# A state-space layer's schedule: one ScalarE table for exp and ln, decays made ahead of Silu, step products and key work at other places

## The chip, the cores and the metric

The kernel runs on one core of a Trainium2 chip. The metric is device time in microseconds (us) from launch to end, the median of three runs. TensorE is PE in the profile (its weight loads PEld), VectorE is DVE, ScalarE is ACT, GpSimd is POOL; SyncE (SP) issues most of the DMAs.

## The reference, cut to what matters

Four layers, each added to `x` (4 x 512 x 512): a selective state-space layer (SSM), a mixture of experts, a cross attention, and a ternary feed-forward. The change is in the first. For each batch `b` of four, with `ctx` (4 x 512 x 256):

```
xs    = in_proj_w @ ctx[b].T                        # 512 channels x 512 steps
u     = silu(causal_conv4(xs, conv_w) + conv_b)
dt_lo, Bm, Cm = split(x_proj_w @ u)                 # 16 rows each
delta = softplus(dt_proj_w @ dt_lo + dt_proj_b)
A     = -exp(A_log)                                 # 512 channels x 16 states
state[e, n] = state[e, n] * exp(delta[e, t] * A[e, n]) + delta[e, t] * u[e, t] * Bm[n, t]
y[e, t]     = sum_n state[e, n] * Cm[n, t] + D[e] * u[e, t]
x[b] += (y * silu(layernorm(x[b]))).T
```

The cross attention also takes `ctx`: its keys (`ctx @ Wk`, 16 heads of 128, RMS normalised) and values (`ctx @ Wv`). Much of these is computed during the SSM, where the kernel has room.

## The kernel before, in words

`ssm_phase` works with channels on the partitions: four chunks of 128 channels (`c`) per batch, 512 time steps along the row. The 16 states of a chunk are done in pairs (`i`, 0 to 7), so a batch is 32 *slots* (`s = c * 8 + i`), and the loop `for q, (b, c, i) in enumerate(seq)` goes through 128 slots, `q` in all. One slot is:

- `inputs` on POOL: `dBu = bb * du`, for two slots ahead (L488; three buffers);
- `decays` on ACT: `dA = exp(delta * A)`, two instructions, one slot ahead (L497; two PSUM buffers, each free when the slot that used it is done on DVE);
- `scan` on DVE: one recurrence over both states (L511), then the product with `cb`, on DVE or, for i = 0, 2 and 4, on POOL (L512; `hc`, three buffers, free when PE has summed them);
- `sums` on PE for the slot before: `hc` is transposed and summed into `yT` (L517). At the second pair of the next chunk or so, `result` multiplies by the gate `gzT` (L551, DVE) and adds to `x_all` (L553, POOL).

Beside it, `ahead(b + 1, s)` prepares the next batch: in slots 0 to 15 the convolution on PE (L304, filters `wcvc` loaded by `load_wcv`, two buffers) and its eviction as `u` (L309); in slot 17 Silu of the four `u` (L376) and layer-norm statistics (`stats`, L380; `norm` on POOL); in 18 and 19 the projection `pd` (L404) and its eviction `xd`; in 20 to 28 four times the *steps*, one for each chunk: product `pdt` (L424) on PE, Abs, Exp and 1+ on ACT (`steps_a`, L428 to L430), Ln (`steps_ln`, L437), and the sum to `delta` on DVE with `du` on POOL (`steps_b`, L443 to L448). softplus(v) is max(v, 0) + ln(1 + exp(-|v|)), with a correction for rounding. In slot 28 Silu of the layer-normed `x` gives the gates `gz` (L397); in 26 to 31 `rows` loads the broadcast `bb` and `cb`. Batch 0 does its own first step ahead of the loop and the other three in slots 2 to 13.

The same slots carry the attention's values (a product `pv` in every odd slot, L470, evicted as `v` in the next even one, L476) and keys: `task` is the product `pk` (L1094), `evict` takes it twice (square into tile `e`, scaled into tile `wt`; L1103, L1104), `squares` sums the squares into `kpss` (L1114), `take` evicts that (L1126) and stores it.

All this is under a manual schedule: every engine runs its instructions in the order in which the program writes them, and waits for those of other engines. A table load on ACT (ACT_TABLE_LOAD) is put in by the compiler wherever a function is not in the loaded set; Exp and Ln are each loaded from a set of their own. PSUM banks are shared by tags: `pa` by `pd`, `pdt`, the gate's transposes `pgz` and key tiles; `pin` by the convolution, key products, and `ln` from batch 1 on (for batch 0 `ln` is in SBUF). After the SSM comes `route`, whose first statistics (L158) reuse the SSM's memory.

Of the kernel before, what the change touches and what calls it, by code (L numbers as in the profile page):

```python
# [17 lines left out]
F32 = mybir.dt.float32  # L18
# [5 lines left out]
AF = mybir.ActivationFunctionType  # L24
# [199 lines left out]


@with_exitstack
def ssm_phase(ctx, cm, x_all, w, kv, dr):
# [11 lines left out]
    KC = CTX // P  # L239
    NP = DS // 2  # L240
    R = 64

# [37 lines left out]
    nc.scalar.dma_start(dtT[0:DR, :], w["dt_proj_wT"])  # L280
    nc.scalar.dma_start(dtT[DR:, :], w["dt_proj_b"])
    nc.scalar.activation(negA, negA, AF.Exp)

# [54 lines left out]
    def silu_0(c):  # L338
        nc.scalar.activation(st[0]["u"][c], st[0]["u"][c], AF.Silu)


# [32 lines left out]
    def silu_u(b):  # L374
        for u in st[b]["u"]:
            nc.scalar.activation(u, u, AF.Silu)  # L376

    def stats(b, c):
# [14 lines left out]
    def silu_gz(b):  # L393
        s = st[b]
        for c in range(NC):
            gz = pool[5].tile([P, S], F32, name="gz")
            nc.scalar.activation(gz, x_all[:, b * NC + c, :], AF.Silu, bias=s["nmr"][:, c:c + 1],  # L397
                                 scale=s["rstd"][:, c:c + 1])
            s["gz"].append(gz)

    def project(b):
# [17 lines left out]

    def steps_a(b, c):  # L420

        s = st[b]
        pdt = s["pdt"] = ps.tile([P, S], F32, name="pdt", tag="pa")
        nc.tensor.matmul(pdt, dtT[:, c * P:(c + 1) * P], s["xd"][0:DR + 1, :], start=True,  # L424
                         stop=True)
        e, wt = (pool[1].tile([P, S], F32, name=n) for n in ("e", "wt"))
        s["e"], s["wt"] = e, wt
        nc.scalar.activation(e, pdt, AF.Abs)  # L428
        nc.scalar.activation(e, e, AF.Exp, scale=-1.0)
        nc.scalar.activation(wt, e, AF.Identity, bias=cm.ones[:, 0:1])  # L430

    def steps_ln(b):

        s = st[b]
        s["ln"] = (pool[5].tile([P, S], F32, name="ln", tag="gz") if b == 0 else
                   ps.tile([P, S], F32, name="ln", tag="pin"))
        nc.scalar.activation(s["ln"], s["wt"], AF.Ln)  # L437

    def steps_b(b, c):

        s = st[b]
        e, wt, ln = s["e"], s["wt"], s["ln"]
        nc.vector.scalar_tensor_tensor(e, wt, 1.0, e, ALU.subtract, ALU.subtract)  # L443
        nc.vector.tensor_tensor(e, ln, e, ALU.subtract)
        delta = pool[5].tile([P, S], F32, name="delta")
        nc.vector.scalar_tensor_tensor(delta, s["pdt"], 0.0, e, ALU.max, ALU.add)
        du = pool[5].tile([P, S], F32, name="du")
        nc.gpsimd.tensor_tensor(du, delta, s["u"][c], ALU.mult)  # L448


        nc.gpsimd.memset(delta[:, 0:1], RESET)
        s["delta"].append(delta)
        s["du"].append(du)
# [36 lines left out]

    def decays(q):
        if q < len(seq):
            b, c, i = seq[q]
            dAs[q] = pda.tile([P, 2, S], F32, name="dA")
            for j in range(2):
                n = 2 * i + j
                nc.scalar.activation(dAs[q][:, j, :], st[b]["delta"][c], AF.Exp,  # L497
                                     scale=negA[:, c, n:n + 1])
# [56 lines left out]
    def ahead(b, s):  # L555

        if s % 4 == 0 and 4 <= s <= 16:
            take_conv(b, s // 4 - 1)
        if s < 16:
            conv(b, s // 4, (s % 4 * 2, s % 4 * 2 + 1))  # L560
        if s in (4, 8):
            load_wcv(b, s // 4 + 1)
        if s == 17:
            silu_u(b)
            for c in range(NC):
                stats(b, c)
            norm(b)
        if s == 18:
            project(b)
        if s == 19:  # L570
            take_project(b)
        if s in (22, 24, 26, 28):
            steps_b(b, (s - 22) // 2)
        if s in (20, 22, 24, 26):
            steps_a(b, (s - 20) // 2)
        if s in (21, 23, 25, 27):
            steps_ln(b)
        if s == 28:
            silu_gz(b)
        if s == 20 and b + 1 < B:  # L580
            start(b + 1)
        if s == 20 and b + 1 == B:
            load_ctx(0, again=True)
        if s in (26, 28, 30, 31):
            rows(b, (26, 28, 30, 31).index(s))

    def key_bank(shape, name):
        return ps.tile(shape, F32, name=name, tag="pin" if name == "pk" and keys.wide else "pa")  # L590

# [4 lines left out]
    def key_steps(b, s, ends):  # L596

        if b > 0 and not ends and s == 0:
            keys.take()
        if b < B - 1:  # L600
            for j, at in enumerate((14, 17, 29) if b == 0 else (3, 6, 11, 14, 17, 29)):
                if not ends and s == at - 3:
                    keys.load(j, j + 1, pool[2], "k_w")
                if not ends and s == at + 3:
                    keys.take()
                if ends and s == at:
                    keys.wide = at > 16
                    keys.task(b + 1, j)
                if ends and s == at + 1:
                    keys.evict()  # L610
                if ends and s == at + 2:
                    keys.squares()
        if b == B - 2 and ends and s in (18, 22):
            h = s - 18
            keys.load(h, h + HG, pool[2], "wcvc")
        if b == B - 1:
            h = s // 2
            if not ends and s % 2:
                keys.take()

            if ends and s == 31:
                keys.squares()
            if ends and s % 2:
                keys.evict()
            if ends and s % 2 == 0:
                if s < 30:
                    keys.squares()
                keys.wide = True
                keys.task(0, h)
                if h in (HG, 2 * HG):  # L630
                    keys.load(h + HG, h + 2 * HG, pool[2], "wcvc")

    def start(b):
        load_ctx(b)
        load_wcv(b, 0)
        load_wcv(b, 1)

# [29 lines left out]
    norm(0)  # L667
    steps_a(0, 0)
    steps_ln(0)
    steps_b(0, 0)  # L670
    decays(0)
    inputs(0)
    inputs(1)
# [3 lines left out]
    for g in range(1, DS // NG):  # L677
        rows(0, g)
    SL = NC * NP
    for q, (b, c, i) in enumerate(seq):  # L680
# [10 lines left out]
        if q % SL == 8 and b + 1 < B:  # L691
            load_x(b + 1)
        if q in (4, 6, 13):
            steps_b(0, len(st[0]["du"]))
        if q in (2, 4, 11):
            steps_a(0, len(st[0]["du"]))
        if q in (3, 5, 12):
# [14 lines left out]
        last = (b + 1) % B, q % SL // 2  # L712
        sums(q - 1)
        key_steps(b, q % SL, True)
    sums(len(seq) - 1)
    take_values(*last)
    keys.take()
    keys.squares()
    keys.take()
# [1563 lines left out]
```

## Time and profile before

Three runs: 2748.58, 2750.00 and 2751.31 us. The profiled execution took 2754.55 us, and its span from first to last instruction is 2752.8.

| stretch of the profiled execution | us |
|---|---|
| before the first scan | 40.2 |
| slots 0 to 15 / 16 to 31 of batch 0 (preparing batch 1) | 74.3 / 78.4 |
| slots 0 to 15 / 16 to 31 of batch 1 | 62.6 / 78.4 |
| slots 0 to 15 / 16 to 31 of batch 2 | 62.3 / 80.0 |
| batch 3, to route's first statistics | 113.4 |
| experts, attention, feed-forward | 2163.2 |

A row of the profile's groups names the line, engine, operation and tiles (out<-in), then shapes and count, busy us and mean ns of one, and the engine's idle time ahead of them with what ended it. A row of waits names who waited for whom, us in total, times, and the longest. A row of the timeline has start, duration, engine and line. Times in the text without another word are us on the profile's own clock.

### The profile page before, as it was taken

What the parts mean: (1) busy time and instruction counts of PE and PEld (TensorE: products, weight loads), DVE (VectorE), ACT (ScalarE), POOL (GpSimd) and SP (SyncE); (2) the same over time, 40 slices, a digit from 0 to 9 for tenths busy, and PEclk for the clock granted to TensorE, in tenths of its full rate; (3) what the DMA queues carried; (4) which work ended last, traced back from release to release, by engine and by line L of the source; (5) the groups of instructions that cost most, each with busy time, mean ns of one, the idle gap of its engine ahead of it and who ended that gap; (6) DMA issues with size and microseconds to landing.
All of it is one profiled execution on the core that took longest, in us unless ns stands there. A gap on an engine that the chain in (4) does not pass through costs nothing. (4 is left out here: it accounts for less than half of the span.)

```text
span 2752.8 us, 30001 instructions
## 1 busy us (share of the span) xinstructions
PE 2545.1 (92%) x10158; PEld 1441.3 (52%) x10158; DVE 1486.0 (54%) x2570; ACT 1275.9 (46%) x2371; POOL 1170.6 (43%) x1121
## 2 busy tenths in 40 slices
PE   5989897976799999999998799999999999999997
PEld 2545454643456666666674455445555554555543
DVE  5887877966432234334423555545665666544445
ACT  6676757743323222222322344445555555555543
POOL 4888887952333244444433423223431443111212
PEclk8979797986899999999999899999999999999999
DMA  6253535322556566879976344324322443221200
GB/s 244 82 201 102 196 103 181 128 78 80 190 187 199 162 216 222 267 264 339 311 235 204 116 134 135 96 88 126 119 92 81 126 126 103 78 81 53 63 31 20
DMA packets 198543, 403.11 MB, mean 146 GB/s; under 512 B 30563, under 2 KB 72099, under 8 KB 194288
## 3 DMA queue, kind: packets, MB, share of 16 engines
q1 hardware_dynamic: 155758, 247.76, 26.9%
q0 software_dynamic: 40576, 153.19, 17.5%
q8 instruction: 83, 1.36, 0.2%
q14 instruction: 76, 0.62, 0.1%
q10 hardware_dynamic: 2050, 0.18, 0.1%
HBM read 319.13 MB, written 81.92 MB: 146 GB/s over the span
## 5 line engine op out<-in xcount | busy, mean ns | idle before, releaser
L1848 DVE TENSOR_REDUCE mx<-psc 128x1 f32<-128x512 f32 x256 | 176.7, 690 | 458.1 <-PE psc L1845 454.8
L1194 PE MATMUL pg<-xT,wg 128*128 128x284 f32 (+12 forms) x1536 | 403.1, 407 | 1.7 <-ACT xT L1181 1.1
L1194 PEld LDWEIGHTS pg<-xT,wg 128*128 128x128 f32 x1536 | 284.5, 195 | 82.7 <-issue 32.0
L1851 ACT ACTIVATE e<-psc,mx 128x512 f32<-128x512 f32 x256 | 176.0, 687 | 313.5 <-DVE mx L1848 313.2
L488 POOL TENSOR_TENSOR dBu<-bb,du 128x1024 f32<-128x1024 f32 x128 | 299.5, 2360 | 26.5 <-DVE dA L511 19.8
L1845 PE MATMUL psc<-kT,qT 128*128 128x512 f32 x512 | 267.0, 603 | 1.0 <-ACT qT L1839 1.0
L1135 POOL DMA_INDIRECT xg<-xn_dram,tok x168 | 172.2, 1025 | 221.6 <-PE pt L1178 179.2
L1872 PE MATMUL po<-eT,v 128*128 128x512 f32 x512 | 233.2, 598 | 9.4 <-ACT eT L1866 9.4
L1811 PE MATMUL pq<-Wq,xnT 128*128 128x512 f32 x512 | 233.3, 599 | 0.7 <-issue 0.7
L1881 PE MATMUL px<-Wo,oT 128*128 128x512 f32 x512 | 231.9, 596 | 0.0
L511 DVE TENSOR_TENSOR_SCAN dA<-dA,dBu 128x1024 f32<-128x1024 f32 x80 | 183.1, 2289 | 56.8 <-ACT dA L497 46.3
L1865 PEld LDWEIGHTS pet<-ident,e 128*128 128x128 f32 x1024 | 127.8, 142 | 146.2 <-issue 120.1
L1822 POOL TENSOR_SCALAR qms<-qms 128x4 f32<-128x4 f32 x64 | 25.0, 391 | 411.5 <-DVE qms L1820 410.7
L497 ACT ACTIVATE dA<-delta,negA 128x512 f32<-128x512 f32 x256 | 176.5, 692 | 18.1 <-DVE hc L512 12.0
L470 PE MATMUL pv<-Wv,ctxb 128*128 128x512 f32 x256 | 148.0, 708 | 28.6 <-ACT v L476 28.6
L517 PEld LDWEIGHTS yT<-ident,hc 128*128 128x128 f32 x1024 | 130.0, 153 | 83.0 <-issue 57.8
L1239 DVE COPY yo<-po 128x512 f32<-128x512 f32 x68 | 47.0, 691 | 231.9 <-PE po L1228 231.8
L1872 PEld LDWEIGHTS po<-eT,v 128*128 128x128 f32 x512 | 96.8, 191 | 136.7 <-issue 116.6
L1865 PE MATMUL pet<-ident,e 128*128 128x128 f32 x1024 | 155.3, 275 | 7.2 <-DVE e L1857 7.2
L1735 POOL DMA_INDIRECT yg<-y_dram,pos x124 | 124.1, 1001 | 87.3 <-issue 63.1
L517 PE MATMUL yT<-ident,hc 128*128 128x128 f32 x1024 | 145.2, 292 | 11.1 <-POOL hc L512 6.4
L1135 POOL DMA_INDIRECT wd<-down,widx x64 | 63.1, 986 | 216.1 <-PE po L1228 182.2
(354 smaller groups left out, 4489.0 us busy)
## 6 DMA issues: line engine op xcount, KB each, us to landing
y_dram<-yo SPq DMA_DIRECT2D x110, 256.0 KB
bb<-bc_dram SPq DMA_DIRECT2D x16, 1024.0 KB
cb<-bc_dram SPq DMA_DIRECT2D x16, 1024.0 KB
v_dram<-v SPq DMA_DIRECT2D x64, 256.0 KB
k_dram<-k_kT SPq DMA_DIRECT2D x64, 256.0 KB
Wq<-Wq SPq DMA_DIRECT2D x16, 1024.0 KB
kT<-k_dram SPq DMA_DIRECT2D x64, 256.0 KB
rk<-r_dram SPq DMA_DIRECT2D x64, 256.0 KB
```

The costliest lines, as they stand in the source:

```text
L488: nc.gpsimd.tensor_tensor(dBus[q], st[b]["bb"][i // 2][:, j:j + 2, :], st[b]["du"][c].unsqueeze(1).to_broadcast([P, 2, S]), ALU.mult)
L497: nc.scalar.activation(dAs[q][:, j, :], st[b]["delta"][c], AF.Exp, scale=negA[:, c, n:n + 1])
L511: nc.vector.tensor_tensor_scan(*flat, 0.0, ALU.mult, ALU.add)
L517: nc.tensor.matmul(yT[:, lc, :], t[:, lc * P:(lc + 1) * P], cm.ident, is_transpose=True, start=first and lc == 0, stop=last, skip_group_ch ...
L1135: nc.gpsimd.indirect_dma_start(out=t[0:n, :], out_offset=None, in_=table, in_offset=bass.IndirectOffsetOnAxis(ap=index, axis=0))
L1194: nc.tensor.matmul(pg[:, 0:n], s["wg"][:, c, m * P:(m + 1) * P], s["xT"][:, c, 0:n], start=c == 0, stop=c == NC - 1)
L1811: nc.tensor.matmul(pq.rearrange("p h d -> p (h d)"), xnTs[b * NC + i][:, c, :], s["Wq"][:, c, :], start=c == 0, stop=c == NC - 1)
L1845: nc.tensor.matmul(pscore, st[b, g]["qT"][:, h, i * P:(i + 1) * P], ks[n], start=True, stop=True)
L1848: nc.vector.tensor_reduce(mx, pscore, AX.X, ALU.max, negate=True)
L1865: nc.tensor.transpose(pt[:, kc, :], e[:, kc * P:(kc + 1) * P], cm.ident)
L1872: nc.tensor.matmul(po, v[:, kc, :], eT[:, kc, :], start=kc == 0, stop=kc == KB - 1)
L1881: nc.tensor.matmul(px, oTs[j * HG + h][:, i * P:(i + 1) * P], st[b, g]["Wo"][:, h, :], start=h == 0, stop=h == HG - 1)
```

## The change

- `tables` loads the set `natural_log_exp_and_others`, which has both Exp and Ln, at the start and after each group of Silu; the compiler then puts in no load between Exp and Ln.
- `steps_a` loses its product, which moves to `dt`, issued a slot earlier: for the first chunk at the end of slot 19, ahead of the key's squares, for the others in slots 21, 23 and 25 ahead of `values` and `sums`. Relu of `pdt` joins Abs on ACT, so that `pdt` is free after these two; `delta` is then relu + e, on DVE, and no longer max(pdt, 0) + e. 1+ moves from `steps_a` to `steps_ln`.
- `steps_b` moves ahead by a slot, to the end of 21, 23, 25 and 27; `du` stays where it was (`step_du`).
- `decays` of slots 18 and 30 are made at the end of 16 and 28, into SBUF buffers of the filters (tag `wcvc`). `load_wcv` for the next batch moves from slot 20 to the ends of 29 and 31.
- `stats` move from slot 17 to 12 to 15, `norm` to 16, Silu of `gz` from 28 to 29.
- Keys: the tasks of slots 3, 6, 11 and 14 move to 2, 5, 10 and 13; each eviction comes a slot later, at its slot's start, and `take` goes to its slot's end. Banks are chosen by task. In batch 3 evictions move from the end of odd slots to the start of even ones, and the weights of heads 4 to 7 are loaded in slot 6 of batch 3 and not in slot 22 of batch 2.

In experts, attention and feed-forward nothing changes. The core of the diff (beside it: calls of `tables(nc)` after the other Silu groups, the same moves for batch 0 ahead of and in its loop, and the last key's eviction after the loop):

```diff
+def tables(nc):
+    nc.scalar.preload_act_table_set("natural_log_exp_and_others")
...
     def silu_u(b):
         for u in st[b]["u"]:
             nc.scalar.activation(u, u, AF.Silu)
+        tables(nc)
...
-    def steps_a(b, c):
+    def dt(b, c):
+        pdt = st[b]["pdt"] = ps.tile([P, S], F32, name="pdt", tag="pa")
+        nc.tensor.matmul(pdt, dtT[:, c * P:(c + 1) * P], st[b]["xd"][0:DR + 1, :], start=True,
+                         stop=True)
+
+    def steps_a(b):
         s = st[b]
-        pdt = s["pdt"] = ps.tile([P, S], F32, name="pdt", tag="pa")
-        nc.tensor.matmul(pdt, dtT[:, c * P:(c + 1) * P], s["xd"][0:DR + 1, :], start=True,
-                         stop=True)
-        e, wt = (pool[1].tile([P, S], F32, name=n) for n in ("e", "wt"))
-        s["e"], s["wt"] = e, wt
-        nc.scalar.activation(e, pdt, AF.Abs)
-        nc.scalar.activation(e, e, AF.Exp, scale=-1.0)
-        nc.scalar.activation(wt, e, AF.Identity, bias=cm.ones[:, 0:1])
+        pdt = s.pop("pdt")
+        s["e"], s["wt"] = (pool[1].tile([P, S], F32, name=n) for n in ("e", "wt"))
+        s["relu"] = pool[5].tile([P, S], F32, name="delta")
+        nc.scalar.activation(s["e"], pdt, AF.Abs)
+        nc.scalar.activation(s["relu"], pdt, AF.Relu)
+        nc.scalar.activation(s["e"], s["e"], AF.Exp, scale=-1.0)

     def steps_ln(b):
         s = st[b]
+        nc.scalar.activation(s["wt"], s["e"], AF.Identity, bias=cm.ones[:, 0:1])
...
-    def steps_b(b, c):
+    def steps_b(b):
...
-        delta = pool[5].tile([P, S], F32, name="delta")
-        nc.vector.scalar_tensor_tensor(delta, s["pdt"], 0.0, e, ALU.max, ALU.add)
+        delta = s.pop("relu")
+        nc.vector.tensor_tensor(delta, delta, e, ALU.add)
+        s["delta"].append(delta)
+
+    def step_du(b):
+        s = st[b]
+        c = len(s["du"])
+        delta = s["delta"][c]
         du = pool[5].tile([P, S], F32, name="du")
         nc.gpsimd.tensor_tensor(du, delta, s["u"][c], ALU.mult)
...
-    def decays(q):
-        if q < len(seq):
+    def decays(q, early=False):
+        if q < len(seq) and q not in dAs:
             b, c, i = seq[q]
-            dAs[q] = pda.tile([P, 2, S], F32, name="dA")
+            dAs[q] = (pool[2].tile([P, 2, S], F32, name="dA", tag="wcvc") if early else
+                      pda.tile([P, 2, S], F32, name="dA"))
...
     def ahead(b, s):
...
+        if 12 <= s < 16:
+            stats(b, s - 12)
+        if s == 16:
+            norm(b)
         if s == 17:
             silu_u(b)
-            for c in range(NC):
-                stats(b, c)
-            norm(b)
...
-        if s in (22, 24, 26, 28):
-            steps_b(b, (s - 22) // 2)
-        if s in (20, 22, 24, 26):
-            steps_a(b, (s - 20) // 2)
+        if s in (20, 22, 24, 26):
+            steps_a(b)
+        if s in (21, 23, 25):
+            dt(b, (s - 19) // 2)
+        if s in (22, 24, 26, 28):
+            step_du(b)
         if s in (21, 23, 25, 27):
             steps_ln(b)
-        if s == 28:
+        if s == 29:
             silu_gz(b)
...
+    def ahead_ends(b, s):
+        if s in (16, 28):
+            decays((b - 1) * SL + s + 2, early=True)
+        if s in (29, 31) and b + 1 < B:
+            load_wcv(b + 1, (s - 29) // 2)
+        if s == 19:
+            dt(b, 0)
+        if s in (21, 23, 25, 27):
+            steps_b(b)
...
     def key_steps(b, s, ends):
...
-            for j, at in enumerate((14, 17, 29) if b == 0 else (3, 6, 11, 14, 17, 29)):
+            for j, at in enumerate((13, 17, 29) if b == 0 else (2, 5, 10, 13, 17, 29)):
-                if not ends and s == at - 3:
+                if not ends and s == max(at - 3, 0):
                     keys.load(j, j + 1, pool[2], "k_w")
-                if not ends and s == at + 3:
+                if not ends and s == at + 2:
+                    keys.evict()
+                if ends and s == at + 3:
                     keys.take()
                 if ends and s == at:
-                    keys.wide = at > 16
+                    keys.banks = {17: ("pin", "pin"), 29: ("pin", "pa")}.get(at, ("pa", "pa"))
                     keys.task(b + 1, j)
-                if ends and s == at + 1:
-                    keys.evict()
                 if ends and s == at + 2:
                     keys.squares()
```

In the loop `ahead_ends(b + 1, s)` follows `sums(q - 1)` and comes ahead of `key_steps(b, s, True)`.

## The prediction, made before the changed kernel ran

> **What bounds the kernel now.** I first read the busy time by stretch, cut where the SSM's slots show it: the scans number the slots, 32 to a batch; the rows are the two halves of batch 0, of batch 1 and of batch 2, and then batch 3 with its tail. Columns: stretch, its length, busy us of PE, weight loads, DVE, ACT, POOL (with counts), granted clock, DMA share, GB/s.
>
> ```profile
> 40.20:114.50 74.30, 63.22 (x223) 34.09 (x224) 57.00 (x37) 49.26 (x69) 60.31 (x31) 0.88 0.48 179
> 114.50:192.90 78.40, 63.15 (x228) 35.99 (x227) 61.00 (x50) 62.91 (x90) 61.89 (x37) 0.78 0.45 154
> 192.90:255.50 62.60, 62.60 (x278) 37.63 (x277) 49.45 (x29) 33.93 (x58) 54.90 (x25) 1.00 0.43 140
> 255.50:333.90 78.40, 63.45 (x231) 35.55 (x230) 61.02 (x49) 63.16 (x90) 60.53 (x36) 0.78 0.44 156
> 333.90:396.20 62.30, 62.30 (x277) 37.39 (x275) 49.35 (x29) 33.79 (x57) 54.88 (x25) 1.00 0.42 139
> 396.20:476.20 80.00, 64.14 (x228) 35.87 (x227) 61.06 (x50) 62.75 (x90) 60.54 (x36) 0.79 0.43 150
> 476.20:589.60 113.40, 105.59 (x569) 70.99 (x567) 98.40 (x59) 75.57 (x137) 102.38 (x47) 0.99 0.36 121
> ```
>
> A first half (slots 0 to 15, with the next batch's convolution) is PE's: 62.6 of 62.6 at full clock, and its products aren't touched. A second half (16 to 31) belongs to nobody: four engines are each some 61 of 78.4 busy, so about 17 us go in waits. Batch 3 has POOL at 102 of 113, and its slots 112 to 119 take 26.7 us with POOL busy throughout. So the change can win in the three second halves, in batch 0's first half (it holds three of batch 0's own steps) and at the tail.
>
> Then the groups of the SSM's stretch, and the waits of batch 1:
>
> ```profile
> L497 ACT ACT_TABLE_LOAD x23 | 29.5, 1283 | 1.9 <-DVE delta L446 1.5
> L437 ACT ACT_TABLE_LOAD x16 | 20.5, 1283 | 0.2
> L428 ACT ACTIVATE e<-pdt 128x512 f32<-128x512 f32 x16 | 9.6, 598 | 33.1 <-PE pdt L424 33.1
> L488 POOL TENSOR_TENSOR dBu<-bb,du 128x1024 f32<-128x1024 f32 x123 | 287.8, 2361 | 26.5 <-DVE dA L511 19.8 <-DMA bb<-bc_dram 5.5 <-DMA v_dram<-v 1.2
> ```
>
> ```profile
> DVE dA L511 <- ACT dA L497: 16.2, 9, 3.8
> ACT k_sq L1103 <- PE pk L1094: 11.2, 5, 2.5
> ACT e L428 <- PE pdt L424: 6.5, 4, 2.7
> PE pv L470 <- ACT v L476: 8.7, 5, 5.3
> ```
>
> The scans wait for decays (L497); ACT is late with them because it loads tables, and because it stands at the head of its queue for pdt and pk, which PE gives late, itself waiting for ACT's v.
>
> **The table loads.** The program orders have 49 table loads in the SSM before and 17 after: 32 x 1.283 = 41.1 us off ACT. The Trainium skill (ScalarE: Activation LUTs, "What ACT_TABLE_LOAD costs") adds a drain of 1.38 to every load, 2.66 in all, which would make it 85. This trace doesn't show that: at 294.54 a load starts 0.02 after a decay's end, and Ln starts 0.01 after the load. I take 1.3. Added: 16 Relu at some 0.60 (as Abs, L428), 9.6 us.
>
> **The port, which speaks against the change.** The skill (SBUF: State Buffer, "Who interferes with whom") says that a DVE instruction with two SBUF inputs and a GpSimd one that reads SBUF exclude each other for a whole instruction. The timeline of DVE shows it:
>
> ```profile
> 62.48 2.65 DVE L444 TENSOR_TENSOR e<-ln,e 128x512 f32<-128x512 f32 x1
> ...
> 297.59 0.69 DVE L444 TENSOR_TENSOR e<-ln,e 128x512 f32<-128x512 f32 x1
> ```
>
> and so does POOL's:
>
> ```profile
> 64.54 2.79 POOL L512 TENSOR_TENSOR hc<-hc,cb 128x1024 f32<-128x1024 f32 x1
> ...
> 296.98 2.72 POOL L512 TENSOR_TENSOR hc<-hc,cb 128x1024 f32<-128x1024 f32 x1 [1.56 <-DVE hc L511]
> ```
>
> With ln in SBUF (batch 0) L444 stands until POOL's instruction ends at 64.5, 2.65 in place of 0.69; with ln in PSUM (297.59) POOL may run beside it. POOL's hc, 2.35 alone, takes 2.7 to 2.8 where it meets L443 (wt and e, both SBUF). The change makes more of that kind: the delta sum now adds relu and e, both SBUF (L446 read pdt from PSUM, 0.69), and the early decays lie in SBUF, so scans 18 and 30 and the product after scan 30 have two SBUF inputs. Without the rule a delta sum costs 0.7; with it, 0.7 to 3.1. I take the rule, since these rows show it, and place each collision below. Behind a blocked DVE instruction stands the next scan; behind a blocked POOL one, dBu and hc.
>
> **A second half, walked on batch 1's clock.** The durations are those of its timeline: scan 2.25, product L512 1.15, dBu 2.33, hc 2.35, two decays 1.42, Silu of u 2.19, v 0.5, a 512-wide PE product 0.86, sums of a slot 0.87.
>
> Slots 16 to 19. The last convolution ends at 258.7 in both. ACT: u, v at 261.1 (after its product), early decays for 18 to 262.5, load, Silu to 266.1, load, decays 19 to 268.8: scan 19 starts there, before at 269.63. The early decays let scan 18 go ahead, but the next scan meets the same Silu. The four stats (3.4 us of DVE, at 263 to 266.5) move to slots 12 to 15, where PE sets the pace: nothing there, and here they lay beside Silu. Scan 18 is blocked by dBu until 265.9; decays 19 hide it.
>
> Slots 19 to 22. pd shares its bank with the gate's, taken by ACT at 269.3 behind decays 19: pd to 272.7, two sums and values to 276.2, pdt to 277.1 (now in front of kpss), kpss to 277.9. Abs writes tile e, which kpss reads, so it starts at 278.0: before 279.57. So this step gains 1.5, not the slot that it moves. Abs, Relu, Exp, v, key's take, decays 22, Identity, Ln: 283.3. L443 starts at 282.75, meets dBu until 283.5; the sum meets the next dBu from 284.95 to 286.5; delta at 287.2. Scan 22 now stands behind delta, where before it stood ahead. Scan 23: 290.8, before 289.1; with no collision 288.4.
>
> Slots 23 to 31. DVE work: 9 scans, 6 products, three steps (2.1 each), one yg: 34.1 us; before these took 44.8, 9.0 of the rest being the waits for decays. After, decays are in time everywhere: Abs, Relu, Exp, v, Identity, Ln and four decays are 6.5 us of ACT in two slots, against 7.8 to 8.9 of DVE work, and Silu of gz (5.4 with its loads, slot 29) hides behind scans 29 and 30, whose decays are made. Collisions: L443 1.15, 0.3, 0.8; delta sums 0, 1.55, 1.6 (the first finds POOL waiting for scan 24); scan 30 0.3, its product 2.4 (dBu goes between); some 0.5 of waiting for dBu: 8.6. Scan 32: 290.8 + 34.1 + 8.6 = 333.5, before 333.9. With no collisions, 288.4 + 34.1 + 1.4 for POOL = 323.9.
>
> PE, however, starts the next first half earlier. Before, values of slot 29 stood 5.33 for v behind gz's Silu, and a backlog put the first convolution product at 335.33. After, v is taken ahead of Silu, and the last sums, released by product 30 (330.1), and kpss put it at 332.0. As PE sets the first half, that is the gain: **3.3** (9 without collisions).
>
> **Elsewhere.** Batch 0's first half: three steps with six loads. u of slot 4, which the next convolution waits for, comes at 66.5 in place of 69.66 (-3.2), and slot 12's wait of 1.42 falls to some 0.6: **4.0**. The loads off the first step (2.6) are worth nothing: dBu of slot 2 starts at 47.93 after bb's landing. Batch 2's second half: batch 3 has no convolution, so the scans count, **0.4**. Batch 3: POOL's. Keys move within PE's slack (6.2 of 6.6 us in two slots); weights of heads 4 to 7, asked for in slot 6 and wanted in slot 8, may cost 0 to 1; 0 taken. Tail: route's first stats wait for the last k_ms to land (589.63); v now goes ahead of the last key's two evictions: **0.9**.
>
> DMAs moved: the filters of the next batch leave slot 20 for 29 and 31 on SP. The first stands behind one pair of bb and cb (2 MB, 5.1 us at the 407 GB/s of 306 to 311), landing 9 us ahead of its use; the second behind cb of slot 31, landing 9 us ahead. Key weights a slot earlier: some 5 us ahead. 0 taken; if that cover goes, PE waits up to 5 a batch.
>
> **Sum.** 4.0 + 3.3 + 3.3 + 0.4 + 0.9 = 11.9. The profiled execution took 2754.55 (span 2752.8, 1.75 around it): 2742.6. The median of the runs is 4.55 below it: **2738**.
>
> **The rivals.**
> - *Collisions fall in POOL's gaps.* For: one of my four sums does. Against: POOL is 61 of 78 busy in a longer half. 4.0 + 9 + 9 + 10 + 0.9 = 33: 2717.
> - *The gain is given back:* a convolution filter or key weights land late, or cold PE (0.5 in half of each second half) eats the 3.3. 2750.
> - *Slower: the port.* A half holds 11 DVE instructions of two SBUF inputs. If they wait 1.7 us each, nearer a whole POOL instruction (2.36), that is 18.7 for the 10.4 that the walk pays: 8.3 more in each of three halves, 25 less 12, so 13 above the median: 2763. It decides from some 14.4 us per half on (4 more, three times). For: POOL nearly always has one queued. Against: delta sums just behind a scan's product often find POOL waiting for that scan.
> - *The change doesn't do what it says:* excluded for loads, since the program has 17.
>
> **How the numbers follow.** First case 0.50 (2728 to 2748), big gain 0.25, given back 0.11, slower 0.14. A measurement here can tell about 0.2%, 5.5 us. Of the first case 0.05 lies within it: faster 0.70, same 0.16, slower 0.14. Range: down to a part of the big gain, 2711, up to the slower one's edge, 2757.
>
> **What would show it.** 17 table loads, no wait for pdt over 1 us; first halves at 62 to 63 us; second halves at 74 to 76 before PE's restart; delta sums with means of 1.5 or more in three of four; scans 30 and 18 longer than 2.3. A mean of 0.7 for the sums would be the big gain; POOL over 65 in a half, the slower case; waits of L304 for wcvc, the third.

## The result, and the profile after

The changed kernel takes 2739.8 us (median of 11 runs, 2733.1 to 2745.75); the kernel before, on the same chip, 2751.3 (11 runs). The ratio is 0.9956, with a 95% interval of 0.9943 to 0.9969: faster by 0.44%, 11.5 us. The profiled execution took 2741.18 us, with a span of 2738.4, against 2754.55 and 2752.8.

The busy time by stretch, cut at the same scans as before: the two halves of batches 0, 1 and 2, then batch 3 with its tail. Columns: stretch, its length, busy us (and counts) of PE, weight loads, DVE, ACT, POOL, then granted clock, DMA share, GB/s.

```profile
39.40:117.20 77.80, 67.10 (x245) 35.91 (x245) 64.55 (x44) 43.98 (x69) 61.54 (x31) 0.91 0.50 186
117.20:191.00 73.80, 55.34 (x220) 32.14 (x218) 65.88 (x43) 52.19 (x83) 64.23 (x36) 0.84 0.46 157
191.00:254.20 63.20, 63.20 (x272) 37.31 (x273) 52.15 (x37) 36.48 (x61) 57.03 (x26) 1.00 0.43 147
254.20:328.50 74.30, 57.64 (x240) 34.38 (x239) 65.11 (x42) 51.57 (x82) 64.34 (x35) 0.86 0.45 160
328.50:391.10 62.60, 62.60 (x267) 36.66 (x267) 52.13 (x37) 36.59 (x61) 56.98 (x26) 1.00 0.43 144
391.10:465.10 74.00, 59.39 (x239) 35.25 (x238) 65.17 (x41) 51.57 (x82) 64.04 (x35) 0.82 0.48 161
465.10:578.50 113.40, 104.30 (x555) 69.46 (x554) 98.38 (x59) 74.03 (x136) 104.54 (x48) 1.00 0.38 119
```

The second halves went from 78.4, 78.4 and 80.0 to 73.8, 74.3 and 74.0. ACT lost about 11 us of work in each, as it should with the loads gone. But DVE gained 4 to 5 us of busy time in each, and POOL 2 to 4: DVE is now busy for 65 of 74. And batch 0's first half became 3.5 longer.

The groups of the SSM's stretch (engine, operation, count, busy us, mean ns, then the engine's idle time ahead of it and what ended it):

```profile
L228 ACT ACT_TABLE_LOAD x9 | 11.5, 1283 | 5.6 <-DMA v_conv_b<-conv_b 5.5
L443 ACT ACTIVATE e<-pdt 128x512 f32<-128x512 f32 x16 | 9.6, 597 | 44.9 <-DVE delta L462 22.2 <-PE pdt L434 11.4 <-PE kpss L1155 11.3
L462 DVE TENSOR_TENSOR delta<-delta,e 128x512 f32<-128x512 f32 x16 | 22.2, 1390 | 0.5
L509 POOL TENSOR_TENSOR dBu<-bb,du 128x1024 f32<-128x1024 f32 x128 | 314.1, 2474 | 21.4 <-DVE dA L534 13.5 <-DMA bb<-bc_dram 7.8
```

With the eight loads ahead of the Silus (L346, L385, L407) the SSM has 17 loads. Abs still waits, in sum longer than before (44.9 for 33.1), but half of it for another thing: the delta sum of the chunk before it (L462), which must release tile e. Its 11.4 for pdt lie in batch 0's own first steps; in the second halves it no longer waits for pdt. What ACT waited for between 50 and 580 us (us in total, times, longest), before:

```profile
ACT k_sq L1103 <- PE pk L1094: 45.9, 26, 3.6
ACT e L428 <- PE pdt L424: 31.9, 15, 6.1
ACT dA L497 <- DVE hc L512: 12.0, 13, 2.1
```

and after:

```profile
ACT dA L520 <- DVE hc L535: 71.0, 45, 5.1
ACT e L443 <- DVE delta L462: 22.2, 10, 3.4
ACT k_sq L1144 <- PE pk L1135: 14.5, 9, 2.8
```

More than half of ACT's waiting is now for DVE, to free a decay's buffer (dA) or tile e, where before it was for PE's keys and pdt. DVE's waits for ACT in batch 1's second half are down to two rows:

```profile
DVE dA L534 <- ACT dA L520: 2.7, 1, 2.7
DVE e L459 <- ACT wt L450: 2.5, 1, 2.5
```

And the timeline of DVE (start, us) shows what took the place of the waits:

```profile
279.70 1.35 DVE L459 SCALAR_TENSOR_TENSOR e<-wt,e 128x512 f32<-128x512 f32 x1 [2.49 <-ACT wt L450]
281.15 0.69 DVE L460 TENSOR_TENSOR e<-ln,e 128x512 f32<-128x512 f32 x1
281.88 1.93 DVE L462 TENSOR_TENSOR delta<-delta,e 128x512 f32<-128x512 f32 x1
...
293.37 0.69 DVE L462 TENSOR_TENSOR delta<-delta,e 128x512 f32<-128x512 f32 x1
...
321.91 3.12 DVE L535 TENSOR_TENSOR hc<-dA,cb 128x1024 f32<-128x1024 f32 x1
```

L460, with ln in PSUM, takes 0.69. L462, the same operation on the same size with both inputs in SBUF, takes 1.93, and 0.69 where POOL has nothing under way (293.37). Product 30, with the early decays in SBUF, takes 3.12 for 1.23.

To set kernels side by side I use the stretch from the start of scan 2 to the start of scan 127, taken from DVE's timeline. It leaves out two things that no edit is aimed at and that differ between executions. One is the start: pd took from 3.65 to 4.78 us in 14 profiles, and scan 2 stands behind it. The other is all that follows scan 127: the same code in all 14 but for the last key's evictions, 2162.6 to 2176.9 us long. Busy time of DVE and ACT, and DVE's waits by the engine that ended them, lie within that stretch. Us:

| kernel | scan 2 to 127 | ACT busy | DVE busy | DVE waits for ACT | for POOL | for PE |
|---|---|---|---|---|---|---|
| before | 528.4 | 370.9 | 427.3 | 60.1 | 12.9 | 18.0 |
| changed | 516.7 | 335.8 | 453.4 | 14.2 | 18.6 | 19.3 |
| tables alone (e4) | 525.4 | 330.2 | 427.7 | 57.6 | 13.7 | 16.3 |
| order without tables (e5) | 517.4 | 374.8 | 449.0 | 18.3 | 18.0 | 21.8 |
| steps and keys (e10) | 520.4 | 375.6 | 443.8 | 22.2 | 10.5 | 34.7 |
| pdt late (e9) | 529.4 | 335.1 | 458.1 | 24.2 | 16.2 | 19.7 |
| ln in SBUF (e6) | 535.6 | 336.3 | 470.4 | 18.0 | 16.4 | 19.7 |
| sum in PSUM (e1) | 512.0 | 335.9 | 442.4 | 14.4 | 25.0 | 19.0 |
| statistics in waits (e3) | 510.8 | 335.7 | 451.7 | 8.8 | 13.6 | 25.9 |
| both of these (e7) | 504.7 | 335.1 | 438.7 | 9.3 | 19.6 | 26.2 |

The gain of 11.7 is the first row less the second: 45.9 us less of waiting for ACT; against it 26.1 more of DVE's own time, 5.7 more of waiting for POOL, 1.3 for PE, and about 1 in small gaps.

### The profile page after: what moved, and what is told of

Its sections match the earlier page's. It is cut to its first block, busy times and chain, and to the rows that moved or that the text cites. A ratio compares the mean times of both kernels' runs of the same rounds, so it can differ in the third digit from the quotient of the medians.

```text
span 2738.4 us, 29994 instructions
## 1 busy us (share of the span) xinstructions
PE 2524.7 (92%) x10158; PEld 1429.8 (52%) x10158; DVE 1514.4 (55%) x2570; ACT 1239.3 (45%) x2355; POOL 1188.5 (43%) x1121
## 5 line engine op out<-in xcount | busy, mean ns | idle before, releaser
L509 POOL TENSOR_TENSOR dBu<-bb,du 128x1024 f32<-128x1024 f32 x128 | 314.1, 2474 | 21.4 <-DVE dA L534 13.5
L534 DVE TENSOR_TENSOR_SCAN dA<-dA,dBu 128x1024 f32<-128x1024 f32 x80 | 182.8, 2284 | 24.1 <-POOL dBu L509 18.6
L1907 ACT COPY eT<-pet 128x512 f32<-128x512 f32 x256 | 148.2, 579 | 4.6 <-PE pet L1906 4.5
```

The lines of the kernel that those rows point to most:

```text
L509: nc.gpsimd.tensor_tensor(dBus[q], st[b]["bb"][i // 2][:, j:j + 2, :], st[b]["du"][c].unsqueeze(1).to_broadcast([P, 2, S]), ALU.mult)
L534: nc.vector.tensor_tensor_scan(*flat, 0.0, ALU.mult, ALU.add)
```

## The experiments

Each ratio below is taken against runs of the kernel before in that experiment's own session, whose medians are 2753.8 to 2754.6; dividing the two medians gives up to 0.0025 more than the ratio shown.

### Which part of the change brings the gain

**Tables alone (e4).** The kernel before, with a load by name after each Silu group, and nothing else.

```diff
+    tables(nc)
     nc.scalar.activation(negA, negA, AF.Exp)
...
     for u in st[b]["u"]:
         nc.scalar.activation(u, u, AF.Silu)
+    tables(nc)
...
         s["gz"].append(gz)
+    tables(nc)
```

> The kernel before with one thing of the change: the table for Exp, Ln and the rest is loaded by name after each Silu group, so that the loads between Exp and Ln disappear (32 loads of 1.28 us). Order, Abs, PSUM delta sum, keys, statistics as before. Port theory (the changed kernel's gain is cut by its new collisions): more than the changed kernel gains, 4 on batch 0's first half and 4 to 9 in each second half, the route's first statistics at 559 to 574 in place of 589.6, time 2720 to 2735. Rival (waits for pdt, kpss and Silu bound the half, not ACT's loads): no more than the changed kernel gains, 578 to 586, time 2740 to 2748.

Measured: 2749.3 us, ratio 0.9982 (0.9965 to 0.9998). All 32 loads are gone and ACT is busy for 40.7 us less; scan 2 to scan 127 is 3.0 shorter. (The 538.5 and 538.3 of a later expectation are the same kernels counted from scan 0, with the start in them.) Where the rest went is to be read from ACT's timeline, before and with the tables alone. Before:

```profile
290.72 0.60 ACT L428 ACTIVATE e<-pdt 128x512 f32<-128x512 f32 x1 [2.70 <-PE pdt L424]
...
294.54 1.28 ACT L437 ACT_TABLE_LOAD   x1
...
296.45 1.28 ACT L497 ACT_TABLE_LOAD   x1
...
300.22 0.60 ACT L428 ACTIVATE e<-pdt 128x512 f32<-128x512 f32 x1 [1.05 <-PE pdt L424]
```

Tables alone:

```profile
292.81 0.60 ACT L438 ACTIVATE e<-pdt 128x512 f32<-128x512 f32 x1 [5.21 <-PE pdt L434]
...
302.30 0.60 ACT L438 ACTIVATE e<-pdt 128x512 f32<-128x512 f32 x1 [3.84 <-PE pdt L434]
```

From one Abs to the next it is 9.50 us before and 9.49 without the loads. The wait for pdt in front of each grew by 2.51 and 2.79, about the two loads of a chunk (2 x 1.28 = 2.57). Over all of the stretch from 50 to 580 us Abs's waits for pdt grew from 31.9 to this, by 33.3 for the 40.7 us of loads:

```profile
ACT e L438 <- PE pdt L434: 65.2, 15, 8.7
```

The loads lay in the shadow of that wait. Of my two readings the first falls: taking the loads out without the new collisions brought no large gain. The second, which named waits for pdt, kpss and Silu as the bound, holds; the gain is even smaller than its ranges (route's first statistics at 588.4 for 578 to 586, and 2749.3 for 2740 to 2748).

**The order without the tables (e5).** The changed kernel with `tables` emptied.

```diff
 def tables(nc):
-    nc.scalar.preload_act_table_set("natural_log_exp_and_others")
+    pass
```

> The changed kernel with its order, but without the load by name: 32 of the loads between Exp and Ln come back (49 in the SSM). The loads taken out of the kernel before alone brought 0.3 us from scan 0 to scan 127 (538.5 to 538.3), since ACT then stood longer for pdt. Theory (each needs the other: in the new order pdt is there in time, and ACT's 6.5 us in two slots become 9.1, more than DVE's 7.8 to 8.9): second halves go back to 76 to 79 us, scan 0 to scan 127 to 534 to 540, time 2745 to 2753. Rival (the order alone brings the gain, loads lie in waits here too): halves stay at 74 to 75, scan 0 to 127 at 529 to 531, time 2739 to 2743.

Measured: 2742.5 us, ratio 0.9942 (0.9924 to 0.996), 517.4 for 516.7. Its SSM has 49 loads again, and ACT 374.8 us of work, more than before the change. My theory that each needs the other is refuted: the rival, that the order alone brings the gain, is what the run shows. DVE's waits between 50 and 580 us in this kernel:

```profile
DVE e L459 <- ACT wt L450: 11.2, 6, 2.7
...
DVE dA L534 <- ACT dA L520: 5.4, 2, 2.7
```

and of the kernel before, in the same window:

```profile
DVE dA L511 <- ACT dA L497: 46.3, 26, 4.2
DVE hc L511 <- ACT dA L497: 13.9, 9, 2.9
```

With all loads in place the scans wait for decays twice, where before they did 35 times. And ACT has room for its loads: its own waits for DVE in that window, 71.0 and 22.2 in the changed kernel, become

```profile
ACT dA L520 <- DVE hc L535: 54.3, 32, 3.1
ACT e L443 <- DVE delta L462: 1.6, 4, 0.7
```

so that 37.3 of the 39.0 us that ACT works more come out of them.

**pdt late (e9).** The changed kernel, one table set and all, with each pdt product issued right ahead of its Abs, as before, in place of a slot earlier.

```diff
 def steps_a(b):
+    dt(b, len(s["delta"]))
     pdt = s.pop("pdt")
...
-        if s in (21, 23, 25):
-            dt(b, (s - 19) // 2)
...
-        if s == 19:
-            dt(b, 0)
...
-        if q in (1, 3, 10):
-            dt(0, len(st[0]["delta"]) + (q == 3))
```

> The changed kernel with one table set and all else, but each chunk's pdt product is issued in the slot of its Abs again, right ahead of it, in place of a slot earlier. Theory (the gain is DVE no longer waiting for decays behind an ACT queue that stands for pdt: 60.1 us of waiting for ACT before, 57.6 with the loads out, 14.2 after, 18.3 after with the loads back): waits for ACT return to 30 to 60, scan 2 to scan 127 from 516.7 to 522 to 535 (the collisions stay, so it may end above before's 528.4), time 2745 to 2758. Rival (keys, Silu's place or the early decays carry the gain): 515 to 519, time 2738 to 2742.

Measured: 2753.0 us, ratio 0.9993 (0.9982 to 1.0003), 529.4: the whole gain is gone. The theory's bounds for the sum hold; its bound for the waits (30 to 60) doesn't, since they come to 24.2. The scans wait for decays no more than in the changed kernel (5.4). Of the 12.7 us, 10.0 are waits for ACT, most of them in the steps themselves, and 4.7 DVE's own time (waits for POOL fall by 2.4). Against the kernel before, DVE does wait 36 us less for ACT, but it works 31 longer and waits 5 longer for POOL and PE, so that nothing is left. Some collisions fall worse: the first DVE step of chunk 3 takes 2.9 where it took 1.3, and one in batch 0's second half 4.95 for 2.44. DVE's waits between 50 and 580 us:

```profile
DVE e L460 <- ACT wt L451: 17.8, 8, 3.1
...
DVE dA L535 <- ACT dA L521: 5.4, 2, 2.7
```

**Steps and keys alone (e10).** The kernel before with the new `steps_a`, `dt`, `steps_b` and `step_du` in their new places, and the new `key_steps`. The keys come with it, because by my reading of the program's order the users of pdt's bank would otherwise wait for each other in a ring; no run tests that, and so none separates steps from keys.

```diff
+        if s in (21, 23, 25):
+            dt(b, (s - 19) // 2)
...
+        if s in (21, 23, 25, 27):
+            steps_b(b)
...
-            for j, at in enumerate((14, 17, 29) if b == 0 else (3, 6, 11, 14, 17, 29)):
+            for j, at in enumerate((13, 17, 29) if b == 0 else (2, 5, 10, 13, 17, 29)):
```

> The kernel before with two things of the change: the steps (Relu, pdt a slot ahead, sums at the slot's end) and the keys' slots, which the steps' banks need. Loads, statistics in slot 17, Silu of gz in slot 28, filters and all decays as before. Theory (these two carry the gain, and the statistics, which cost in slots 12 to 15 of batch 0, stay out of it): waits for ACT fall to 15 to 30, scan 2 to scan 127 at 511 to 518, time 2734 to 2742. Rival (the gain needs the other moves as well): 520 to 528, time 2743 to 2752.

Measured: 2742.7 us, ratio 0.9951 (0.9936 to 0.9967), 520.4. The waits for ACT fall to 22.2, within the theory's bounds. The sum is a little outside them (511 to 518), the time too (2734 to 2742): these two bring 8.0 of the 11.7, and the rest of the moves a net 3.7, after what the statistics cost (e3 below). Which of the rest brings it was not tested. No table load is taken out here.

### The port

**The sum out of PSUM (e1).** In batches 1 to 3 the difference stays in ln's bank, so that the delta sum has one SBUF input.

```diff
-        nc.vector.tensor_tensor(e, ln, e, ALU.subtract)
+        to = e if b == 0 else ln
+        nc.vector.tensor_tensor(to, ln, e, ALU.subtract)
         delta = s.pop("relu")
-        nc.vector.tensor_tensor(delta, delta, e, ALU.add)
+        nc.vector.tensor_tensor(delta, delta, to, ALU.add)
```

> The changed kernel, but in batches 1 to 3 the difference ln - e is left in ln's PSUM bank, and the delta sum adds relu to it: one SBUF input less, nothing else moved. Port theory: the three long delta sums of a second half (1.93, 1.92, 1.95 us on batch 1) fall to 0.69, second halves of batches 1 and 2 shorten by 2.5 to 3.7 each (71 to 72 in place of 74), batch 0's likewise; the route's first statistics 8 to 11 us earlier than the changed kernel's 578.8, time 2729 to 2733. Rival (the sum is long for another reason than its inputs, or POOL is what sets these slots): sums stay near 1.9, or they shorten and the halves stay at 74; time 2738 to 2742.

Measured: 2735.8 us, ratio 0.9915 (0.9888 to 0.9941). The timeline of DVE:

```profile
279.43 1.16 DVE L459 SCALAR_TENSOR_TENSOR e<-wt,e 128x512 f32<-128x512 f32 x1 [2.67 <-ACT wt L450]
280.69 0.70 DVE L461 TENSOR_TENSOR ln<-ln,e 128x512 f32<-128x512 f32 x1
281.42 0.69 DVE L463 TENSOR_TENSOR delta<-delta,ln 128x512 f32<-128x512 f32 x1
```

All sixteen sums take 0.69, so their length came from their inputs. DVE's busy time falls by 11.0, which is what the nine long sums of the changed kernel had over that ((1.93 - 0.69) x 9 = 11.2). But the stretch is only 4.7 shorter: DVE waits 6.4 longer for POOL's dBu. Batches 1 and 2 gained 2.8 and 2.1, batch 0's second half nothing (74.0 for 73.8), where one L459 took 4.75 for 2.44. So the theory's mechanism is shown, and its price was too high: the route's first statistics come 5.2 earlier, not 8 to 11. What was won by taking collisions away was given back in part, and the trace says where: the scans then stood for the dBu that POOL had not finished.

**ln in SBUF (e6).** The dose the other way: ln in SBUF in every batch, so that the difference has two SBUF inputs too.

```diff
-        s["ln"] = (pool[5].tile([P, S], F32, name="ln", tag="gz") if b == 0 else
-                   ps.tile([P, S], F32, name="ln", tag="pin"))
+        s["ln"] = pool[5].tile([P, S], F32, name="ln", tag="gz")
```

> The changed kernel with ln in SBUF in all batches, as it is in batch 0's own steps: the difference ln - e has two SBUF inputs as well. Port theory: it meets a POOL instruction as the delta sum does (1.2 us more, up to 1.96 as in batch 0's 2.65), in about three of four: second halves 2 to 5 us longer than 74, scan 0 to scan 127 at 534 to 542 for the 529.2, time 2745 to 2755. Rival (POOL has paid already by then, or its gap is there): L460 stays at 0.69 and nothing changes, 2738 to 2742.

Measured: 2759.0 us, ratio 1.0012 (1.0002 to 1.0023), 535.6: 18.9 more than the changed kernel. The effect has the sign and the place that the port theory gave it, and is larger: the stretch from scan 0, in which the bound is given, is 548.5 (534 to 542), the halves are 5.7, 7.8 and 5.7 longer (2 to 5), and the time is above its range too; 2.2 of the 7.8 is scan 30, which took 4.47. Of the delta sums of a half two also grew, from 1.92 and 1.95 to 2.71, and the first fell from 1.93 to 0.69. On the timeline of DVE, the same three instructions:

```profile
284.21 1.17 DVE L459 SCALAR_TENSOR_TENSOR e<-wt,e 128x512 f32<-128x512 f32 x1 [2.67 <-ACT wt L450]
285.49 2.65 DVE L460 TENSOR_TENSOR e<-ln,e 128x512 f32<-128x512 f32 x1
288.17 0.69 DVE L462 TENSOR_TENSOR delta<-delta,e 128x512 f32<-128x512 f32 x1
```

L460 takes 2.64 to 2.67 in three of four steps of a half. One operand's place (ln) is worth more than the whole change, and between e1 and e6, which differ in two operands (ln and the difference, in PSUM or in SBUF), lie 23.6 us.

**No early decays (e2).**

```diff
-        if s in (16, 28):
-            decays((b - 1) * SL + s + 2, early=True)
```

> The changed kernel without the early decays (slots 18 and 30 take theirs in PSUM at the usual place). My theory: what they bring at scan 18 is hidden by Silu in front of scan 19, and they cost a blocked product 30 (3.12 us for 1.23) and a blocked nmr on POOL: second halves 0 to 2 us shorter, time 2733 to 2740. Rival (early decays carry much of the gain): scans 18, 19 or 31 wait for decays, second halves 2 to 4 us longer, time 2745 to 2752.

Measured: 2732.1 us, ratio 0.9909 (0.9884 to 0.9933), but scan 2 to scan 127 is 515.9 for 516.7. The trace gives the early decays no net worth, as my theory had it. DVE works 9.0 less (5.3 on products: three took 2.8 to 3.1, now none is over 1.4; 3.7 on three delta sums, which no longer meet POOL) and waits 3.6 less for POOL; it waits 5.8 more for ACT and 7.1 more for PE.

The times say more than that: the interval lies clear of the changed kernel's 0.9943 to 0.9969 (that of e12, 0.9929 to 0.997, it just touches), and the medians are 8 to 10 us apart, so the early decays seem to cost time. Of this the trace shows 0.8 in the stretch and 1.1 in the tail: from scan 127 to the route's first statistics it is 9.2 in e2, e10 and e11, which have the new order without early decays, and 9.9 to 10.4 in the nine kernels that have them. Another 5.3 of this profile lies after the tail, in code that is the same, where profiles differ by more than that. The rest is open.

**The changed kernel again (e12).**

> The changed kernel unaltered, beside the others on the same chip: scan 2 to scan 127 within 1 of 516.7, time 2736 to 2744 by every theory; how far the start (pd, 4.71 us for 3.65) and the experts (2159.6) move tells how much of a difference between profiles is theirs.

Measured: 2741.9 us, ratio 0.9949 (0.9929 to 0.997), 518.8 for 516.7, so outside the bound of 1. The 2.2 us lie in one place, scan 30 of batch 1. On its timeline:

```profile
319.33 4.47 DVE L534 TENSOR_TENSOR_SCAN dA<-dA,dBu 128x1024 f32<-128x1024 f32 x1
323.91 3.14 DVE L535 TENSOR_TENSOR hc<-dA,cb 128x1024 f32<-128x1024 f32 x1
```

and in the first profile of the same kernel:

```profile
319.53 2.28 DVE L534 TENSOR_TENSOR_SCAN dA<-dA,dBu 128x1024 f32<-128x1024 f32 x1
321.91 3.12 DVE L535 TENSOR_TENSOR hc<-dA,cb 128x1024 f32<-128x1024 f32 x1
```

POOL's dBu starts at 319.31 in the one and at 319.52 in the other. Where it started 0.02 ahead of the scan, the scan stood until it ended; where it was 0.01 ahead, the scan went through in 2.28 and POOL took longer. The other kernels with early decays bear this out. At scans 18 and 30 of a batch an instruction of POOL (dBu, or the last one of the norm, nmr) starts 0.03 or less ahead of the scan 17 times in the nine profiles: with a lead of 0.007 to 0.015 the scan went first, 9 times, and with 0.016 to 0.026 POOL did, 8 times. So 2.2 us hang on about a hundredth of one.

### The statistics

**Statistics in DVE's waits (e3).** Two in slot 18, two and the norm in slot 21, in place of slots 12 to 16.

```diff
-        if 12 <= s < 16:
-            stats(b, s - 12)
-        if s == 16:
-            norm(b)
...
+        if s in (18, 21):
+            for c in range(2):
+                stats(b, c + 2 * (s == 21))
+        if s == 21:
+            norm(b)
```

> The changed kernel, but the next batch's statistics are taken in slots 18 and 21, two in each, where DVE waits (2.73 and 2.49 us on batch 1, 2.37 and 1.38 on batch 0), and the norm in slot 21. Theory: on batch 0 DVE sets slots 13 to 15 (4.35 us each, 4.2 of it DVE), so that scan 16 comes 2.6 to 3.5 us earlier there, and some 2 of it is kept at scan 32; batches 1 and 2, whose slots 12 to 15 PE sets, don't change: 2 to 3 us earlier at the route's first statistics, time 2736 to 2738. Rival (PE sets those slots on batch 0 as well): no change, 2738 to 2742.

Measured: 2737.0 us, ratio 0.9912 (0.9882 to 0.9941), 510.8: 5.9 less than the changed kernel, twice what I expected. All but 1.0 is batch 0's: from scan 2 to scan 16 it is 62.9 for 65.4, from scan 16 to scan 32 71.4 for 73.8. The changed kernel's slots 14 and 15 of batch 0, on DVE:

```profile
108.52 2.28 DVE L534 TENSOR_TENSOR_SCAN dA<-dA,dBu 128x1024 f32<-128x1024 f32 x1
110.91 1.23 DVE L535 TENSOR_TENSOR hc<-dA,cb 128x1024 f32<-128x1024 f32 x1
112.05 0.69 DVE L390 BATCH_NORM_STATS2 st_a<-x_all 128x6 f32<-128x512 f32 x1
112.77 0.18 DVE L391 BATCH_NORM_AGGREGATE mv<-st_a 128x2 f32<-128x6 f32 x1
112.86 2.28 DVE L534 TENSOR_TENSOR_SCAN dA<-dA,dBu 128x1024 f32<-128x1024 f32 x1
```

and without the statistics there:

```profile
107.39 2.29 DVE L534 TENSOR_TENSOR_SCAN dA<-dA,dBu 128x1024 f32<-128x1024 f32 x1
109.78 1.23 DVE L535 TENSOR_TENSOR hc<-dA,cb 128x1024 f32<-128x1024 f32 x1
110.92 2.29 DVE L534 TENSOR_TENSOR_SCAN dA<-dA,dBu 128x1024 f32<-128x1024 f32 x1
```

DVE works without a gap in both: 4.34 us a slot and 3.53. PE is not what these slots wait for.

### Versions beyond the change

**Both edits (e7), and all of ln in PSUM (e8).** e7 is e1's and e3's edit together. In e8 batch 0's own steps keep ln in pdt's bank as well:

```diff
-        s["ln"] = (pool[5].tile([P, S], F32, name="ln", tag="gz") if b == 0 else
-                   ps.tile([P, S], F32, name="ln", tag="pin"))
+        s["ln"] = s["pdt"] if b == 0 else ps.tile([P, S], F32, name="ln", tag="pin")
```

> Both edits that helped: statistics in slots 18 and 21 (scan 0 to 127: 523.6 for 529.2) and the delta sum out of PSUM (524.5). Theory (they remove different things, batch 0's statistics and batches 1 and 2's sums): they add up to 8 to 10 us, scan 0 to 127 at 519 to 521, time 2728 to 2732. Rival (both shorten the same waits): 522 to 524, time 2733 to 2737.

> As the run with both edits, and batch 0's own steps keep ln in pdt's PSUM bank in place of SBUF, so that no difference and no delta sum has two SBUF inputs. Port theory: the two differences that took 2.65 us in slots 5 and 12 of batch 0 fall to 0.69; of these 3.9 us some 0 to 2 reach the end of that half, since PE is at 23.5 to 24.3 of 25 there: scan 0 to 127 at 517 to 521, time 2726 to 2732. Rival (the bank, held until the sum, makes the next pdt, gate and key wait): the half grows by 1 to 3, 2731 to 2736.

Measured: e7 2729.7 us, ratio 0.9899 (0.9882 to 0.9916), 504.7: 12.0 less than the changed kernel, the sum of both (4.7 + 5.9) and a little over, and past both readings' bounds (from scan 0 it is 517.5). It beats both kernels; its interval lies clear of the changed kernel's, 0.9943 to 0.9969. e8: 2731.9 us, 0.9917 (0.9901 to 0.9934), 504.3. The two differences of 2.65 fall to 0.70 as the port has it, and 0.9 of the 3.9 shows up to scan 16; 0.5 of it is lost again by scan 32. The two can't be told apart.

**Both edits without early decays (e11).** e7 with e2's edit.

> Statistics in slots 18 and 21, the delta sum out of PSUM, and no early decays. Theory (early decays bring nothing net: 515.9 for 516.7 without them): scan 2 to scan 127 within 2 of 504.7, time 2727 to 2732. Rival (with the collisions gone they are what lets scan 18 and 30 go): 507 to 511, time 2733 to 2737.

Measured: 2727.0 us, ratio 0.9896 (0.9862 to 0.993), 507.1. By the stretch the early decays are worth 2.4 here, just past the theory's bound and just within the rival's; the time is the theory's (2727 to 2732). The two don't agree, as in e2, and the medians of e7 and e11 can't be told apart.

## Why the prediction was right, and which steps were not

The forecast was 2738 us, faster by 0.5%; it is 2739.8. Forecast was a gain of 11.9; the medians differ by 11.5, and in the profiles the SSM ends 10.8 earlier (11.7 between scans 2 and 127, 0.7 at the tail, less 1.6 for a later start). Its parts are not, and one reason behind it fails. The direction was understood, waits for ACT going and collisions coming; that the sum agrees so closely is luck. From batch 0 to batch 1 it fell short by 3.4 and in batch 3 by 1.0, and batch 2 made that up with 3.9 more.

**What it said of ACT: half right.** It held that the scans wait for decays because ACT "loads tables, and because it stands at the head of its queue for pdt and pk". The second clause carries nearly everything. Loads alone bring 3.0 us of the stretch (e4), loads put back cost 0.7 (e5, less than the 2.2 between two profiles of one kernel), and a late pdt costs 12.7 (e9). The loads' 41 us was counted correctly and was worth next to nothing, in the old order because ACT stood for pdt longer by nearly as much, in the new one because ACT waits for DVE and so has room.

What made that room is shown only in part: the steps and the keys together (e10). The early product is needed for the gain (e9). But it is not what keeps the decays in time, since in e9 the scans wait for them for 5.4 us as well. A rival for that is the keys' new slots: ACT's waits for pk fell from 45.9 to 14.5 and for kpss from 33.9 to 13.6, both more than the 31.9 that it waited for pdt, and in e9 they stay down (12.3 and 12.2). The Relu takes pdt out of its bank early; before, the next product stood 13.5 us for the delta sum (L446) that held the bank:

```profile
L424 PE MATMUL pdt<-xd,dtT 17*128 17x512 f32 x32 | 20.3, 716 | 15.1 <-DVE delta L446 13.5 <-ACT k_ms L1126 0.8 <-ACT xd L409 0.8
```

That the product can go a slot ahead because of the Relu is argued from this; no run leaves the Relu out. The walk counted it only as a cost of 9.6.

**Batch 0's first half, 4.0: reached PE and went no further.** The convolution from first to last product took 70.5 for 75.0, so 4.5 at that point. But the half's own end, scan 16, came 1.2 later, counted from scan 2.

**Batch 0 to batch 1, 3.3: nothing.** From the last convolution product in batch 0's slots to the first in batch 1's it is 77.0 for 76.9. The step that failed is the statistics "to slots 12 to 15, where PE sets the pace: nothing there". That was read from batches 1 and 2 and carried to batch 0, where after its own steps DVE sets those slots. Their price there is 3.5 of DVE work, and 5 by scan 32 (e3, where the interval named above is 70.8 for 77.0; e10, which keeps them in slot 17, shows the same 62.9 up to scan 16).

**Batch 1 to batch 2, 3.3: 3.8.** The walk was exact on its clock where its mechanism was right. With 3.05 for the earlier start of the half added, scan 19 stands at 268.8 (forecast 268.8), Abs at 278.6 (278.0), scan 23 at 290.3 (290.8), the convolution's first product at 331.6 (332.0).

**Collisions, 10.4 a half: 8.1.** The rule of the Trainium skill (SBUF — State Buffer, "Who interferes with whom") agrees with every row shown here; sizes were off. L459 0.68, 1.08, 0.10, 0.63 (forecast 0.75, 1.15, 0.3, 0.8); the delta sums 1.24, 0, 1.23, 1.26 (1.55, 0, 1.55, 1.6), so I was right that the second finds POOL waiting; product 30 1.9 (2.4); scan 30 nothing in the profile, 2.2 in e12. Scan 18 I had blocked by POOL; it was the other way, and POOL's nmr beside it took 2.31 for 0.23. The page says that the order of issue decides who blocks. The 17 meetings at e12 agree down to a lead of some 0.015 us on the profile's clock; below that the scan went, though POOL's start is recorded first. As a cost the 8.1 is not what the half loses: e1 took away 3.7 of a half and got 2.1 to 2.8. One row was misread: POOL's hc at 64.54 meets L444, since L443 had ended at 62.4; L444 too has two SBUF inputs there, so the argument stands.

**Batch 2, 0.4: 4.3.** The 0.4 was batch 1's difference (333.9 less 333.5). Batch 2's own second half, in a row shown there, was 80.0 where batch 1's was 78.4: 1.6 of it was in plain view. The other 2.3 is just what the collisions came out smaller; that this counts fully here, where no PE restart hides it, is arithmetic and not shown (in this batch e1 got 2.1 for 3.7).

**Batch 3, 0: it lost 0.95.** Scan 96 to scan 127 is 102.44 to 102.53 in the kernels before, e2, e4 and e10, and 103.40 to 103.47 in all that have early decays, which the batch itself does not use. That points to POOL, held up behind product 30 and entering batch 3 with work left over; e11, without early decays, has 103.1, so the cause is not settled.

**Tail, 0.9: 0.7.** Right, and without early decays it is 1.8 (e2, e10).

**The rivals.** "Slower: the port" did not come, but its mechanism is no phantom: with one more operand in SBUF the kernel is at 2759 (e6), four below the 2763 that I had worked out, and nothing is left of the gain. "Collisions fall in POOL's gaps" is excluded by three long sums in four. Keys, filters and weights landed in time: between 50 and 580 us no row of PE's waits names a DMA.

## What to carry to other kernels

Before a load or any other fixed cost is taken out of an engine, look at what that engine waits for in the same period: if it stands there for a product that another engine delivers late, the cost can come back as a longer wait (here 33.3 of 40.7 us), and what brought the gain was the order of the work. Two SBUF inputs on DVE beside a busy POOL cost here from nothing to 4.3 us (L459 in e9), nearly two dBu of POOL. A PSUM bank for one of them is worth asking for, but what comes back is less than the collisions' own time: 4.7 of 11.0 us in e1, because POOL's result was still due. A piece of work that is moved "to where another engine sets the pace" must be placed by the slots of each batch, not by those of one that looks typical.

## What the runs showed that I had not expected

- An interval of 9.50 us between two Abs stayed at 9.49 when 2.57 us of loads left it.
- Two profiles of one kernel differ by 2.2 us at a single scan (2.28 or 4.47 us), after a lead of POOL of 0.01 or 0.02 us; 17 such meetings in nine profiles go the same way. In the five kernels without early decays (before, e2, e4, e10, e11) no scan is over 2.4 us and no product on DVE over 1.4; each of the other nine has long products, and seven of them a long scan as well.
- In e9 and in e1 a single scalar_tensor_tensor of two SBUF inputs took 4.95 and 4.75 us for 0.67. In e1 it starts at 141.18 and ends at 145.93, 0.6 after the second of two dBu of POOL (from 140.71 and 143.01, some 2.36 each): it stood through two instructions, not one.
- The code after scan 127, unaltered in all 14 profiles but for the last key's evictions, took 2162.6 to 2176.9 us. That is more than the change is worth, and a reason to read such a change from its own stretch.
